# Gathered rows turned on VectorE in 32x32 blocks, odd halves grouped in threes: a mixture-of-experts layer on one Trainium2 core

## The chip, the core and the metric

The kernel runs on one core of a Trainium2 chip. The metric is the time of one execution on the device in microseconds (us); of the kernel before, the median of 9 runs is 820.46. In the text PE is the matrix engine (TensorE) and PEld its weight loads, DVE is VectorE, ACT is ScalarE, POOL is GpSimd and SP is SyncE.

## What is computed

Eight sequences of 512 tokens with 256 features pass one cross-attention and one mixture of experts. Everything is fp32. Cut to what matters:

```
x = x + tanh(g_xattn) * attention(layernorm(x), ctx, ctx, mask)      # 16 heads of 16
x_flat = layernorm(x).reshape(4096, 256)
probs = softmax(x_flat @ router_w + router_b)                        # 8 experts
top_w, top_idx = top_k(probs, 2)
for e in range(8):
    h = gelu(x_flat @ expert_up[e].T)                                # 256 -> 1024
    out_e = h @ expert_down[e].T                                     # 1024 -> 256
    output = output + comb[:, e:e+1] * out_e                         # comb: top_w where e was chosen, else 0
x = x + tanh(g_ffn) * output
```

Each token goes to two experts, so 8,192 rows have to be taken through an expert's two matmuls.

## The kernel before

**Attention first, experts behind it.** `attend_near` takes the eight sequences (batches) one after the other; four stages per batch, each in three parts, hold the attention's steps, and `plan` and `amid` place other work into them by hand. After a batch's attention its rows are normalised and written to a DRAM tensor `rows`, the sum so far goes to `out` (L309 and L312), the router's top two are found (L319 to L356), and `place` (L370 to L390, on POOL) works out for each token the line of a DRAM `table` that it goes to. `enter` (L394) writes the entries with eight indirect DMAs per batch, two per 128 tokens. The table has a share for each expert, filled from its beginning.

**Groups.** A half is 128 rows of one expert, that is 128 lines of the table. A job is a group of halves that one expert works on: a pair (256 rows) or a single (128 rows). Jobs 0 to 4 are full pairs that exist after batch 3 and jobs 5 to 16 full pairs that exist after batch 6. Then come 15 pairs and, after every third of them up to four times, a single that takes an expert's odd last half. `plan` (L642 to L692, small DVE operations) works out which expert and which line each job has, before any of them runs. `JOBS` lists 36 jobs that always run, `MAIN` of them; `compute_extra` holds up to four more singles under a condition that is read at the end.

**One job.** `list_rows` (L712, SP) reads the job's token numbers and weights out of the table. `load` (L724 and L725, SP) brings the expert's two weight matrices, 1 MB each, in one of three buffers. `fetch` (L730, POOL) gathers the rows of the tokens, one indirect DMA per half, into `xg`. `turn` (L746) transposes them on PE, four transposes of 128x128 for a pair, into a PSUM bank, and DVE copies the bank to `xT` (L748). `go_up` (L758) multiplies by the up weights, and ACT applies Gelu (L762) into `hT`. `fetch_y` (L730 as well) gathers what `out` holds for these tokens. `go_down` (L776) multiplies by the down weights, one half at a time, DVE adds the weighted result to the gathered rows (L779), and POOL scatters them back to `out` (L782). As a token's second expert must see the first one's sum, a job's gather from `out` waits until the scatters of the job before have landed.

**Order.** A matmul of fp32 shows as two records in the trace. Jobs 0 to 3 and the turn of job 4 are placed by hand into batches 4 to 7 (`amid`). From job 4 on `compute` writes out the steps of a job s: the row gather of job s+2, the `out` gather of job s-1, the way up of s in four parts, the turn of s+1, the way down of s-1, the listing of s+3 and the load of s+2. The last job does its own way down at the end. After each step one step is taken from a queue with what is left of batches 6 and 7: the projection, the normalisation, the routing, `place`, `enter` and the plans. Within these dependences a scheduler orders each engine's instructions; the ones marked as kept stay in the program's order. Engines and queues then run in order.

The code before:

Of the kernel before, what the change touches and what calls it, by code (L numbers as in the profile page):

```python
# [35 lines left out]

TOKENS = B * S
GROUP = 2 * P
PAIRS = 2 * TOKENS // GROUP
SINGLES = E  # L40

TABLE = TOKENS // GROUP


PARTS = (3, 6, B, B)
ENDS = [-(-(b * S * 2 - E * (GROUP - 1)) // GROUP) for b in PARTS[:2]] + [PAIRS]
SIZES = [ENDS[0], ENDS[1] - ENDS[0], ENDS[2] - ENDS[1], SINGLES]

OFTEN = SINGLES // 2

TABLES = E * TABLE + SIZES[2]

# [3 lines left out]
for _n in range(SIZES[2]):  # L56
    JOBS.append((2, _n))
    if _n % 3 == 2 and _n // 3 < OFTEN:
        JOBS.append((3, _n // 3))
MAIN = len(JOBS)  # L60
JOBS += [(3, n) for n in range(OFTEN, SINGLES)]
# [3 lines left out]
def flamingo_layer(ctx: ExitStack, tc: tile.TileContext, a: dict, out: bass.AP):  # L65
# [11 lines left out]
    table = tc.dram_tile([TABLES * GROUP, ENTRY], I32, name="table")  # L77

    table_parts = dram_disjoint_views(table, B * QT * 2)
    out_parts = dram_disjoint_views(out, 2)  # L80
# [73 lines left out]
    def clear_table(t):  # L154

        many = t.rearrange("p (n c) -> p n c", c=ENTRY)[:, : TABLES * GROUP // P // 11]
        nc.gpsimd.memset(many, 0)
        nc.gpsimd.memset(many[:, :, 0], TOKENS)
        nc.gpsimd.memset(many[:, :, 1], TOKENS - 1)
        n = many.shape[1]  # L160
        nc.sync.dma_start(
            out=table.rearrange("(p r n) c -> p r (n c)", p=P, n=n),
            in_=t[:, : n * ENTRY].unsqueeze(1).to_broadcast([P, TABLES * GROUP // P // n, n * ENTRY]),
        )
# [8 lines left out]
    full_i = mk.tile([P, 2 * TABLE], I32, tag="full_i", name="full_i")  # L173
    nc.gpsimd.iota(full_i, pattern=[[P, 2 * TABLE]], base=0, channel_multiplier=0)
    full = fixed([P, 2 * TABLE], "full")
# [13 lines left out]
    nc.vector.tensor_scalar(filled, iota, float(TOKENS), None, ALU.mult)  # L189
# [422 lines left out]
    def experts(pool, seen, half_bank, bank, row_bank):  # L612
# [6 lines left out]
        tables, loaded, fetched, turned, made, ys = {}, {}, {}, {}, {}, {}  # L619

        def halves(s):
            return 1 if JOBS[s][0] == 3 else 2

        def plan(k):
            n = SIZES[k]
            single = k == 3
            w = 1 if single else 2
            lines = 2 * TABLE // w

            def planned(shape, name, dtype=F32):  # L630
                return plans.tile(shape, dtype, tag=f"{name}{k}", name=f"{name}{k}")

            def scratch(shape, name):
                return plans.tile(shape, F32, tag=name, name=f"{name}{k}")

            def count():

                count = scratch([P, E], "count")
                nc.vector.scalar_tensor_tensor(count, iota, -float(TOKENS), filled, ALU.mult, ALU.add)  # L642
                if not single:
                    nc.vector.tensor_scalar(count, count, 1.0 - GROUP if k < 2 else -float(P), None, ALU.add)
                more = scratch([P, E, lines], f"more{lines}")
                nc.vector.tensor_tensor(
                    more, count.unsqueeze(2).to_broadcast([P, E, lines]),
                    full[:, ::w].unsqueeze(1).to_broadcast([P, E, lines]), ALU.is_gt,
                )
                groups = scratch([P, E + 1], "groups")  # L650
                nc.vector.memset(groups[:, E:], 0.0)
                nc.vector.tensor_reduce(groups[:, :E], more, AX.X, ALU.add)
                if k:
                    nc.vector.scalar_tensor_tensor(groups, tables["done"], -2.0 / w, groups, ALU.mult, ALU.add)
                ahead = scratch([P, E + 1, E], "ahead")
                nc.vector.tensor_tensor(
                    ahead, lower, groups[:, :E].unsqueeze(1).to_broadcast([P, E + 1, E]), ALU.mult
                )
                begin = scratch([P, E + 1], "begin")
                nc.vector.tensor_reduce(begin, ahead, AX.X, ALU.add)  # L660

                line = scratch([P, E + 1], "line")
                nc.vector.scalar_tensor_tensor(line, iota_e, float(lines), begin, ALU.mult, ALU.subtract)
                if k:
                    nc.vector.scalar_tensor_tensor(line, tables["done"], 2.0 / w, line, ALU.mult, ALU.add)
                past = scratch([P, n, E + 1], f"past{n}")
                nc.vector.tensor_tensor(
                    past, slot[:, :n].unsqueeze(2).to_broadcast([P, n, E + 1]),  # L670
                    begin.unsqueeze(1).to_broadcast([P, n, E + 1]), ALU.is_ge,
                )
                whose = scratch([P, n], f"whose{n}")
                nc.vector.tensor_reduce(whose, past, AX.X, ALU.add)
                whose_i = planned([P, n], "whose_i", I32)
                nc.vector.tensor_scalar(whose_i, whose, -1.0, float(E - 1), ALU.add, ALU.min)
                nc.vector.tensor_tensor(past, past, line.unsqueeze(1).to_broadcast([P, n, E + 1]), ALU.mult)
                far = scratch([P, n], f"far{n}")
                nc.vector.tensor_reduce(far, past, AX.X, ALU.max)
                line_i = planned([P, n], "line_i", I32)  # L680
                nc.vector.tensor_tensor(line_i, far, slot[:, :n], ALU.add)
                tables[k] = (whose_i, line_i, planned([P, n, w, FIELDS], "listed", I32))
                if single:
                    tables["extra"] = planned([P, 1], "extra", I32)
                    nc.vector.tensor_scalar(tables["extra"], begin[:, E:], float(OFTEN), None, ALU.is_gt)
                else:
                    done = planned([P, E + 1], "done")
                    nc.vector.tensor_scalar(done, begin, -1.0, float(n), ALU.mult, ALU.add)
                    nc.vector.tensor_scalar(done, done, 0.0, None, ALU.max)
                    nc.vector.tensor_tensor(done, done, groups, ALU.min)  # L690
                    if k:
                        nc.vector.tensor_tensor(done, done, tables["done"], ALU.add)  # L692
                    tables["done"] = done

            return count
# [11 lines left out]
        def list_rows(s):  # L707
            _, line_i, listed, n = planned_for(s)
            w = halves(s)
            lines = E * 2 * TABLE // w + SIZES[JOBS[s][0]]  # L710
            line = number(line_i, n, lines - 1)
            nc.sync.dma_start(  # L712
                out=listed[:, n],
                in_=table[: lines * w * P].rearrange("(r h p) c -> p r h c", h=w, p=P)[
                    :, bass.ds(line, 1), :, :FIELDS
                ].rearrange("p o h c -> p (o h) c"),
            )
# [16 lines left out]

        def fetch(s):
            xg = gather.tile([P, 2, D], F32, tag="xg", name=f"xg{s}")
            for h in range(halves(s)):
                rows_of(rows, s, h, xg[:, h, :])
            fetched[s] = xg

        def turn(s):
            xg, w = fetched.pop(s), halves(s)
            ps = row_bank(f"x_ps{s}").rearrange("p (c r) -> p c r", c=DC)
            for dc in range(DC):
                for h in range(w):
                    nc.tensor.transpose(ps[:, dc, h * P : (h + 1) * P], xg[:, h, dc * P : (dc + 1) * P], ident)  # L746
            xT = gather.tile([P, DC, GROUP], F32, tag="xT", name=f"xT{s}", bufs=2)
            nc.vector.tensor_copy(xT[:, :, : w * P], ps[:, :, : w * P])  # L748
            turned[s] = xT

        def go_up(s, f):
            up, xT, n = loaded[s][0], turned[s], halves(s) * P
            if f == 0:
                made[s] = hpool.tile([P, FC, GROUP], F32, tag="hT", name=f"hT{s}")
            ps = half_bank(f"h_ps{s}_{f}").rearrange("p (i r) -> p i r", i=2)
            for i in range(2):
                for dc in range(DC):
                    nc.tensor.matmul(  # L758
                        ps[:, i, :n], lhsT=up[:, dc, (f + i) * P : (f + i + 1) * P], rhs=xT[:, dc, :n],
                        start=(dc == 0), stop=(dc == DC - 1),  # L760
                    )
            nc.scalar.activation(made[s][:, f : f + 2, :n], ps[:, :, :n], AF.Gelu)  # L762

        def fetch_y(s):

            ys[s] = gather.tile([P, 2, D], F32, tag="y", name=f"y{s}", bufs=2)
# [20 lines left out]
        def ups(s):  # L787
            return [lambda f=f: go_up(s, f) for f in range(0, FC, 2)]
# [4 lines left out]
        def compute(s, end, first):  # L793
# [4 lines left out]
            steps += ups(s)  # L798
            if s + 1 < end:
                steps.append(lambda: turn(s + 1))  # L800
            if s > first:
                steps += downs(s - 1)
# [8 lines left out]
        def compute_extra():  # L811
            some = nc.values_load(
                tables["extra"][0:1, 0:1], min_val=0, max_val=1, skip_runtime_bounds_check_because="it is a comparison"
            )
            with tc.If(some == 1):
# [627 lines left out]
```

## Time and profile before

| what | value |
|---|---|
| median of 9 runs (lowest to highest) | 820.46 us (816.39 to 826.05) |
| the profiled execution | 816.49 us |
| its span, first to last instruction | 814.7 us |
| mean granted PE clock | 0.976 |
| busy: PE, PEld | 750.9 us (92%), 561.8 us (69%) |
| busy: DVE, ACT, POOL | 320.6 us (39%), 253.9 us (31%), 311.9 us (38%) |
| way up, L758, pairs and singles | 1152 matmul records |
| way down, L776 | 1088 matmul records |
| turns on PE, L746 | 136 transposes |
| row gathers, `out` gathers, scatters on POOL | 68 each |

The profiled execution's own time is 1.8 us more than its span; the median of the runs is 4 us above it. A matmul's busy time is modelled and overlaps with the next, so the time that a run of matmuls really takes is read from the chain of work or from the starts in the timeline. The attention lasts until about 361 us; the last batch's normalisation and routing run until about 389 us beside the first of the jobs from 4 on, and from there on the experts are alone.

### The profile page before, as it was taken

What the parts mean: (1) busy time and instruction counts of PE and PEld (TensorE: products, weight loads), DVE (VectorE), ACT (ScalarE), POOL (GpSimd) and SP (SyncE); (2) the same over time, 40 slices, a digit from 0 to 9 for tenths busy, and PEclk for the clock granted to TensorE, in tenths of its full rate; (3) what the DMA queues carried; (4) which work ended last, traced back from release to release, by engine and by line L of the source; (5) the groups of instructions that cost most, each with busy time, mean ns of one, the idle gap of its engine ahead of it and who ended that gap; (6) DMA issues with size and microseconds to landing.
All of it is one profiled execution on the core that took longest, in us unless ns stands there. A gap on an engine that the chain in (4) does not pass through costs nothing.

```text
span 814.7 us, 11329 instructions
## 1 busy us (share of the span) xinstructions
PE 750.9 (92%) x4090; PEld 561.8 (69%) x4090; DVE 320.6 (39%) x958; ACT 253.9 (31%) x487; POOL 311.9 (38%) x420
## 2 busy tenths in 40 slices
PE   4989989896999999899986999999999999999992
PEld 1443444443465757578875888888898988989881
DVE  6867988789865485442400111111111101111100
ACT  3464646372664344524211111212111121111210
POOL 2030124425363434555463535342444334443331
PEclk9998999899999999999998999999999999999997
DMA  4700102000762230526357665756576675766611
GB/s 156 264 8 3 63 27 82 27 29 29 269 213 93 79 108 26 183 79 193 123 185 256 201 225 187 241 175 215 185 236 197 241 222 183 266 200 211 206 47 37
DMA packets 87910, 121.58 MB, mean 149 GB/s; under 512 B 16798, under 2 KB 71713, under 8 KB 87841
## 3 DMA queue, kind: packets, MB, share of 16 engines
q1 hardware_dynamic: 75184, 93.44, 34.2%
q0 software_dynamic: 11840, 26.76, 10.6%
q8 instruction: 36, 0.59, 0.3%
q10 hardware_dynamic: 816, 0.53, 0.2%
q14 instruction: 34, 0.27, 0.1%
HBM read 101.05 MB, written 20.17 MB: 149 GB/s over the span
## 4 chain that ended last, share of the span: by engine, by line
PE 44%; DMA 3%; issue 2%; POOL 2%; DVE 0%; SPq 0%; POOLq 0%
PE o_ps L776 21%; PE h_ps L758 21%; PE x_ps L746 1%; DMA out<-y,listed 1%; DMA up<-in_upT 1%; POOL table L394 1%; DMA table<-entries,place_i 1%; POOL y L730 1%; DMA y<-out,listed 0%; POOL out L782 0%; POOL xg L730 0%; DMA listed<-table 0%; DVE y L779 0%; POOL filled L371 0%; POOL place L370 0%
## 5 line engine op out<-in xcount | busy, mean ns | idle before, releaser
L776 PE MATMUL o_ps<-down,hT 128*128 128x256 f32 x1088 | 243.5, 382 | 8.1 <-DVE y L779 6.9
L758 PE MATMUL h_ps<-xT,up 128*128 128x256 f32 (+1 forms) x1152 | 243.9, 368 | 3.3 <-DVE tops L890 1.7
L776 PEld LDWEIGHTS o_ps<-down,hT 128*128 128x128 f32 x1088 | 204.9, 191 | 39.6 <-DVE y L779 7.4
L758 PEld LDWEIGHTS h_ps<-xT,up 128*128 128x128 f32 x1152 | 208.1, 190 | 33.8 <-issue 4.7
L762 ACT ACTIVATE hT<-h_ps 128x512 f32<-128x512 f32 (+1 forms) x144 | 82.3, 573 | 359.0 <-PE h_ps L758 359.0
L779 DVE SCALAR_TENSOR_TENSOR y<-o_ps,listed,y 128x256 f32<-128x256 f32 x68 | 32.6, 483 | 262.2 <-DMA y<-out,listed 162.9
L730 POOL DMA_INDIRECT y<-out,listed x68 | 66.3, 974 | 163.9 <-DMA out<-y,listed 130.5
L782 POOL DMA_INDIRECT out<-y,listed x68 | 68.8, 1012 | 90.8 <-DVE y L779 65.0
L890 DVE TENSOR_REDUCE tops<-t_ps 128x4 f32<-128x512 f32 x128 | 79.2, 681 | 13.1 <-PE t_ps L885 13.0
L730 POOL DMA_INDIRECT xg<-rows,listed x68 | 64.9, 954 | 41.6 <-issue 16.5
L920 ACT ACTIVATE n_pT<-w_ps 128x512 f32<-128x512 f32 x128 | 66.9, 597 | 39.0 <-PE w_ps L915 38.9
L394 POOL DMA_INDIRECT table<-entries,place_i x64 | 62.7, 980 | 25.7 <-issue 16.5
L748 DVE COPY xT<-x_ps 128x512 f32<-128x512 f32 (+1 forms) x36 | 23.7, 659 | 115.8 <-PE x_ps L746 115.8
L915 PE MATMUL w_ps<-ql,km 32*128 32x512 f32 x256 | 51.8, 677 | 1.4 <-DVE tops L890 1.4
L954 PE MATMUL proj_ps<-woT,oT 128*128 128x256 f32 x128 | 33.1, 394 | 10.7 <-DVE oT L947 10.7
L885 PE MATMUL t_ps<-k,q 32*128 32x256 f32 x512 | 41.5, 404 | 1.1 <-ACT q L557 0.8
L867 POOL TENSOR_TENSOR x<-x,bo 128x1024 f32<-128x1024 f32 x8 | 18.9, 2370 | 59.3 <-issue 34.0
L885 PEld LDWEIGHTS t_ps<-k,q 32*128 32x128 f32 x512 | 25.8, 184 | 20.8 <-issue 11.8
L954 PEld LDWEIGHTS proj_ps<-woT,oT 128*128 128x128 f32 x128 | 23.2, 192 | 22.0 <-DVE oT L947 12.7
L933 PE MATMUL n_av<-n_pT,nv 128*32 128x512 f32 x256 | 35.8, 633 | 1.7 <-DVE xT L748 1.7
L939 DVE STREAM_TRANSPOSE raw<-n_av 128x512 f32<-128x512 f32 x32 | 22.8, 712 | 32.1 <-PE n_av L933 31.0
L553 PE MATMUL q_ps<-n_xnT,wqT 128*128 128x512 f32 x64 | 33.3, 645 | 0.8 <-ACT n_xnT L282 0.5
(187 smaller groups left out, 542.2 us busy)
## 6 DMA issues: line engine op xcount, KB each, us to landing
up<-in_upT SPq DMA_DIRECT2D x36, 1024.0 KB, 7.7
down<-in_downT SPq DMA_DIRECT2D x36, 1024.0 KB, 6.2
out<-x SPq DMA_DIRECT2D x8, 512.0 KB, 3.2
rows<-xn_f SPq DMA_DIRECT2D x8, 512.0 KB, 3.6
x<-in_x SPq DMA_DIRECT2D x7, 512.0 KB, 6.9
table<-none SPq DMA_DIRECT2D x1, 2288.0 KB, 12.1
xg<-rows,listed POOLq DMA_INDIRECT x68, 4.4
y<-out,listed POOLq DMA_INDIRECT x68, 2.8
```

The costliest lines, as they stand in the source:

```text
L394: nc.gpsimd.indirect_dma_start(out=table_parts[2 * t + i][:, :], out_offset=bass.IndirectOffsetOnAxis(ap=place_i[:, t, i : i + 1], axis=0) ...
L730: nc.gpsimd.indirect_dma_start(out=dst, out_offset=None, in_=src[: seen[JOBS[s][0]], :], in_offset=bass.IndirectOffsetOnAxis(ap=listed[:, ...
L758: nc.tensor.matmul(ps[:, i, :n], lhsT=up[:, dc, (f + i) * P : (f + i + 1) * P], rhs=xT[:, dc, :n], start=(dc == 0), stop=(dc == DC - 1),)
L762: nc.scalar.activation(made[s][:, f : f + 2, :n], ps[:, :, :n], AF.Gelu)
L776: nc.tensor.matmul(ps, lhsT=hT[:, f, h * P : (h + 1) * P], rhs=down[:, f, :], start=(f == 0), stop=(f == FC - 1))
L782: nc.gpsimd.indirect_dma_start(out=out_parts[h][:, :], out_offset=bass.IndirectOffsetOnAxis(ap=listed[:, n, h, 0:1], axis=0), in_=y[:, h, ...
L885: ins = nc.tensor.matmul(ps[j][:, u], lhsT=q[rows_j, c, t * P : (t + 1) * P], rhs=k[rows_j, c], start=True, stop=True)
L890: nc.vector.tensor_reduce(top[:, 2 * tp : 2 * tp + 2, :].rearrange("p t (i x) -> p t i x", i=2)[:, :, :, 32 * j], ps[j], AX.X, ALU.max,)
L915: ins = nc.tensor.matmul(ps[j], lhsT=km[rows_j, c, i, :], rhs=lowered[b, c][rows_j, i, :], start=True, stop=True)
L920: nc.scalar.activation(pT[:, j, :], ps[j], AF.Exp)
L933: ins = nc.tensor.matmul(av[32 * j : 32 * j + 32, :], lhsT=made_of(b)[3][:, 8 * c + 2 * j + r, :], rhs=pT[:, j, :], start=True, stop=True,)
L954: nc.tensor.matmul(ps[:, t - ts[0], :], lhsT=outs[b, c][:, t * P : (t + 1) * P], rhs=w["woT"][:, c, :], start=(c == 0), stop=(c == DC - 1),)
```

## The change

**Turns.** From job 4 on rows are no longer transposed on PE. `turn_block` uses DVE's transpose, which turns blocks of 32x32. A step i reads 32 partitions of `xg` and does four transposes that write to the four groups of 32 partitions of `xT`; the access patterns put each block at its place in the transposed matrix. Four such steps, 16 instructions, turn a job's rows from SBUF to SBUF. In `compute` they stand one behind each part of the way up. Jobs 0 to 3 keep the turn on PE.

**Groups of three.** The singles are gone. Of the rows that are left after job 16, an expert with an odd number of halves and at least two pairs left gives its last three halves as a triple (384 rows); at most four triples, the rest in pairs. `JOBS` has 32 jobs that always run: 5 + 12 pairs as before, then 11 pairs with a triple after the second, fifth, eighth and eleventh; seven more pairs stand under conditions. A triple's way up takes eight parts of one 128-row weight block by 384 columns. A triple has buffers of its own (`wide`), in memory that the attention's buffers leave when the queue of leftover steps is empty. The table becomes one list of lines of 128 rows, with a share of 33 per expert, and a job reads two or three lines from wherever it begins. The plans are rewritten for this; the third and fourth become one, `plan_rest`.

**The last job.** Its way up is split: a quarter of it, then the way down of the job before, then the rest, then its own way down.

The diff, cut:

```diff
-PAIRS = 2 * TOKENS // GROUP
-SINGLES = E
-PARTS = (3, 6, B, B)
-SIZES = [ENDS[0], ENDS[1] - ENDS[0], ENDS[2] - ENDS[1], SINGLES]
-OFTEN = SINGLES // 2
+TRIPLES = 4
+HALVES = TOKENS // P
+SHARE = HALVES + 1
+PARTS = (3, 6, B)
+SIZES = [ENDS[0], ENDS[1] - ENDS[0], TRIPLES, 2 * TOKENS // GROUP + E - 1 - TRIPLES - ENDS[1]]
+OFTEN = SIZES[3] - 7
+MORE = OFTEN + 3
+LINES = E * SHARE + 2 * SIZES[3]
...
-for _n in range(SIZES[2]):
-    JOBS.append((2, _n))
-    if _n % 3 == 2 and _n // 3 < OFTEN:
-        JOBS.append((3, _n // 3))
+for _n in range(OFTEN):
+    JOBS.append((3, _n))
+    if _n % 3 == 1 and _n // 3 < TRIPLES:
+        JOBS.append((2, _n // 3))
...
         def halves(s):
-            return 1 if JOBS[s][0] == 3 else 2
+            return 3 if JOBS[s][0] == 2 else 2
...
+        def plan_rest():
+            count = count_rows(2)
...
+            nc.vector.tensor_reduce(pairs, more[:, 0], AX.X, ALU.add)
+            nc.vector.tensor_reduce(whole, more[:, 1], AX.X, ALU.add)
+            left, odd = each("left"), each("odd")
+            nc.vector.tensor_tensor(left, pairs, tables["done"][:, :E], ALU.subtract)
+            nc.vector.tensor_tensor(odd, pairs, whole, ALU.subtract)
+            three = each("three")
+            nc.vector.scalar_tensor_tensor(three, left, 2.0, odd, ALU.is_ge, ALU.mult)
...
+        def turn_block(s, i):
+            w = halves(s)
+            if i == 0:
+                where, bufs = (wide[0], 1) if w == 3 else (gather, 2)
+                turned[s] = where.tile([P, DC, w * P], F32, tag="xT" if w == 2 else "xT3", name=f"xT{s}", bufs=bufs)
+            src = fetched[s].rearrange("p h (k g x) -> p g k h x", k=DC, x=32)
+            dst = turned[s].rearrange("p k (h i r) -> p i k h r", h=w, r=32)
+            for g in range(4):
+                nc.vector.transpose(dst[32 * g : 32 * g + 32, i], src[32 * i : 32 * i + 32, g])
...
-        def go_up(s, f):
+        def go_up(s, f, m):
...
-            ps = half_bank(f"h_ps{s}_{f}").rearrange("p (i r) -> p i r", i=2)
-            for i in range(2):
+            ps = half_bank(f"h_ps{s}_{f}")[:, : m * n].rearrange("p (i r) -> p i r", i=m)
+            for i in range(m):
...
         def ups(s):
-            return [lambda f=f: go_up(s, f) for f in range(0, FC, 2)]
+            m = 512 // (halves(s) * P)
+            return [lambda f=f: go_up(s, f, m) for f in range(0, FC, m)]
+        def turns(s):
+            return [lambda i=i: turn_block(s, i) for i in range(4)]
...
-            steps += ups(s)
+            up = ups(s)
+            last = downs(s - 1) if s > first else []
             if s + 1 < end:
-                steps.append(lambda: turn(s + 1))
-            if s > first:
-                steps += downs(s - 1)
+                turned_next = turns(s + 1)
+                for step in up:
+                    steps += [step, *turned_next[:1]]
+                    turned_next = turned_next[1:]
+                steps += turned_next + last
+            else:
+                steps += up[:2] + last + up[2:]
...
-            + [lambda: load(5), lambda: turn_rows(4)],
+            + [lambda: load(5), *turns(4)],
...
                 if queue:
                     queue.popleft()()
+                    if not queue:
+                        heads.close()
+                        open_wide()
```

## The prediction

> **What bounds the kernel now.** I read the profiled execution first by the page's busy shares, then by stage, then along the chain of work that ended last. The execution took 816.49 us: its span of 814.7 and 1.8 around it. The median shown is 820.46, so sums are made on 816.49 and the same difference is taken off the median.
>
> The page says that PE is busy for 92% of the span. An average hides where the rest is, so the next view is the busy time by stretch (columns: stretch; its length; PE, PEld, DVE, ACT and POOL busy with their counts; granted clock; DMA share; GB/s):
>
> ```profile
> 400.00:427.00 27.00, 25.30 (x120) 21.72 (x119) 6.84 (x33) 4.18 (x7) 16.08 (x17) 1.00 0.48 151
> 427.00:441.33 14.33, 7.59 (x37) 6.50 (x37) 0.54 (x2) 2.39 (x4) 5.58 (x6) 0.87 1.03 361
> 441.33:785.20 343.87, 343.87 (x1693) 304.39 (x1694) 40.10 (x75) 58.08 (x103) 140.06 (x143) 1.00 0.61 203
> ```
>
> From 441.33 to 785.20 PE never stops: 343.87 of 343.87 us at clock 1.00, with DVE 12% busy. This is the expert stage once the attention is over. Before it lies a hand-over with holes. The same stretch in the chain of work (start, length, what) has PE instructions alone:
>
> ```profile
> 578.30 6.91 PE h_ps L758 x32
> 585.20 0.22 PE x_ps L746 x2
> 585.42 6.91 PE o_ps L776 x32
> 592.33 3.57 PE h_ps L758 x32
> 595.90 0.44 PE x_ps L746 x4
> ```
>
> A pair's way up and its way down cost 6.91 us each. The turn that stands between them costs 0.44 (0.22 for a single half). A single's way up costs 3.57, more than half of 6.91, because its 32 weight loads serve 128 columns each. Here every microsecond taken off PE shortens the run, as long as nothing else falls behind it.
>
> **Turns off PE, steady stretch.** From job 4 on `turn` becomes `turn_block`. After 441.33 the chain holds 21 turns at 0.44 and 4 at 0.22: 9.2 + 0.9 = **10.1 us removed**.
>
> **Triples for singles.** The plan changes from 32 pairs and 4 singles to 28 pairs and 4 triples: 68 halves both times. I counted each expert's rows from the inputs: 6, 9, 6, 10, 8, 9, 11 and 9 halves. Four experts have an odd half and at least two pairs left, so each of the four triples is full, and 11 pair groups remain for the 11 places. The conditional groups behind them are skipped, as now. PE's columns stay the same; only the short matmuls go. One up matmul record takes 6.91 / 32 = 0.216 us at 256 columns and 3.57 / 32 = 0.112 at 128, so by the same slope 0.320 at 384 and 10.25 for a triple's way up. Four pairs and four singles cost 4 x (6.91 + 3.57) = 41.9, four triples 41.0: **0.9 removed**. Four loads of 2 MB go as well; they are hidden (DMA share 0.61). Of the edits around them none is on the path: a triple's eight Gelus (between 0.38 at 256 columns and 0.60 at 512) lie beside 10.25 us of PE; the table grows from 36,608 to 38,400 rows and is cleared before the first token is routed; the triples' buffers take the attention's memory, but the first is filled some 13 jobs after the attention ends.
>
> **The blocks on DVE.** The rows that price them (mean ns of one after the bar):
>
> ```profile
> L748 DVE COPY xT<-x_ps 128x512 f32<-128x512 f32 x32 | 22.0, 688 | 92.0 <-PE x_ps L746 92.0
> L947 DVE STREAM_TRANSPOSE oT<-n_o 128x512 f32<-128x512 f32 x16 | 11.4, 710 | 0.5
> 398.51 0.29 DVE L646 TENSOR_TENSOR more<-count,full 128x128 f32<-128x128 f32 x1
> ```
>
> A pair's turn loses one copy of 0.69 and gains 16 transposes over 32 partitions, 128 elements deep. No row shows that form. From below, the small DVE operations of the planning take 0.16; from above, a transpose of 512 elements takes 0.71. I take 0.30, from the nearest row by depth, 128 elements in 0.29. That is 4.8 us per pair, between 2.6 and 11.4. A triple's blocks are 192 deep: 0.37 each, between this row and 0.44 for 256 elements, so 5.9 us.
>
> A pair job will last 2 x 6.91 = 13.8 us on PE. DVE then needs 4.8 + 2 x 0.48 for its two `y` additions = 5.8, and 12.4 at the upper bound. So the cost is nothing, hidden by PE's 13.8 us, unless DVE's order matters. The blocks stand in front of `y` of the job before. That `y` waits for a loop on POOL: scatter, landing, gather of the next `y`, landing. In the last jobs it reads: additions start at 778.30, the second at 778.70; the scatters end at 781.70; the gather starts at 783.93 when they have landed; its second half issues at 785.22 and lands 2.74 later (the chain's last y gather) at 787.96. From addition to the next possible addition: 787.96 - 778.70 = 9.3 us. DVE has nothing else to do in that gap, and 4.8 fits. If the cover is gone (blocks over about 9.3 / 16 = 0.58 each), `y` comes late and PE runs out of its two banks.
>
> The Trainium skill speaks against such blocks. "VectorE: DVE Perf Modes", section "Two Vector instructions with no wait between them", says that an instruction whose input or output starts in another group of 32 partitions than the last one's begins only when everything earlier has finished. All 16 blocks change their output group, so by it none overlaps another, while in this trace two additions of 0.48 took 0.88 together. The same page's section on the fixed extra latency gives (N + 151) / 0.96 ns for an fp32 addition of N elements, an estimate of 291 for 128 and 4.7 us for 16 in a row: the sum would not change. No row of this case shows a change of group.
>
> **The hand-over, 340 to 441 us.** Three things move. First, job 4's blocks now run on DVE amid the last attention work. The second half of its rows landed late (its turn is at 350.8, its way up begins at 353.04). With 4.8 us in place of 0.69 the way up can start some 4 later, with other PE work to fill part: +2.5, between 0 and 5. Second, a job now has 14 steps in place of 11, so the queue that is emptied one step per step puts batch 7's routing and its table writes about half a job earlier against PE. The hole that this may close:
>
> ```profile
> 422.51 4.92 DMA up<-in_upT
> 427.43 0.14 issue
> 427.57 7.14 PE h_ps L758 x32
> 434.71 0.45 PE x_ps L746 x4
> 435.16 5.63 issue
> 440.79 0.49 DVE y L779
> 441.33 8.70 PE o_ps L776 x32
> ```
>
> PE idles 0.83, 0.71, 1.55 and 6.18 here, and after the last hole its 32 matmuls take 8.70 instead of 6.91 (clock 0.87 in that stretch): 11.1 in all, plus 7 turns of 0.44. Third, against it: the table writes bunch. POOL has six indirect issues per job at 1.29 (start to start), 7.7 us; placing takes 4.5 and eight table writes 10.3. In one job of 13.8 that is 22.5, so POOL could fall 8.7 behind, and `y` with it. The planning on DVE is as long as before (about 45 small operations in place of 36). From -14 (11.1 and 3.1 gone) to +9 (POOL's lag, with job 4's loss in the same hole); I take **-2**, near the middle.
>
> **The end.** The last group's `y` gather used to wait for the group before. Now that group's way down comes after a quarter of the last way up, and the gather lands behind the other three quarters (7.7 us) and the first half's way down. Two scatters and three gathers on POOL move forward with it, past no other work; SP has nothing left to issue. Today PE ends at 799.03 and the last scatter is issued until 803.35: 4.32. With `y` there: 0.2 + 0.48 + 0.28 + 1.02 = 2.0. If the last two scatters still wait for one addition, 1.3 comes back. So 1.0 to 2.3; I take **-1.7**.
>
> **Sum:** -10.1 - 0.9 - 2 - 1.7 = -14.7 on 816.49, so 801.8 for a profiled execution. The median goes from 820.46 to **805.8**.
>
> **Rivals.**
> 1. The hand-over decides upward: POOL's bunching and job 4 cost +9 in place of -2, so the sum is -3.7 and the median 816.8. For it: a PE hole of 6.18 came from just such a backlog. Against: part of it only replaces the hole that is there. Chance 0.10.
> 2. The hand-over closes: -14, the sum -26.7, median 793.8. For it: the wait at 435 began with a late weight load behind the table writes, which move earlier. Chance 0.12.
> 3. Slower: DVE's order puts the blocks between the arrival of `y` and its addition, so they lengthen the loop. It becomes 9.3 + 16b against today's period of 14.26 (2 x 6.91 + 0.44). It turns slower from b = 0.31 per block, hardly above my 0.30. At b = 0.40 the loop is 15.7, +1.4 against today for some 18 pair jobs, +26, less 2.6 for the end and the triples: about 844. Against: in program order the blocks come before that addition, with a gap of 9.3 for 4.8. Chance 0.08.
> 4. Nothing gained: PE's matmuls stretch by what the turns leave (granted clock below 1.00 in the steady stretch), 820. The clock is 1.00 now with PE fully busy. Chance 0.04.
>
> **How the numbers follow.** The forecast has 0.66. The range reaches to 796, toward case 2, and to 817, with case 1 inside. What is left out is case 3, case 4 and part of case 2, some 0.2. By 0.5% (4.1 us, about what a measurement of this kernel can tell from no change) the bound for faster is 816.4: the forecast, case 2 and half of case 1 give 0.83; the same 0.09 (half of 1 and case 4); slower 0.08.
>
> **What would show it.** Right: no x_ps on PE after job 3; PE busy for the whole stretch after the hand-over; rows of about 0.3 us for 16 blocks per pair; a triple's way up near 10.25; the last scatter about 2 us behind PE's end. Wrong: PE idle behind DVE `y` in steady pair jobs, or DVE `y` issued late behind xT blocks (rival 3); new holes before the steady stretch (rival 1).

## The result and the profile after

The kernel after takes **859.45 us** (median of 20 runs, 854.03 to 865.87) against 822.72 for the kernel before (62 runs): a ratio of 1.0445, 95% interval 1.0422 to 1.0468. It is slower, where 805.8 was forecast. The profiled execution has a span of 860.2 against 814.7. The profiled execution of before, 816.49, lies near its fastest run (816.39) and 6 us under its median, so a difference between two profiles can be some 6 us off from one between medians.

The busy time by stretch of the kernel after; first the stretch shown of before, then two parts of it (columns as there):

```profile
441.33:785.20 343.87, 307.17 (x1327) 257.95 (x1326) 125.37 (x378) 52.39 (x92) 130.87 (x134) 0.95 0.52 173
443.60:554.00 110.40, 110.40 (x513) 97.17 (x512) 46.87 (x146) 19.11 (x32) 47.97 (x50) 1.00 0.63 210
554.00:785.20 231.20, 194.50 (x805) 158.77 (x804) 76.32 (x225) 33.28 (x60) 82.53 (x85) 0.92 0.48 156
```

PE was busy for all of 343.87 us before and for 307.17 now. The loss has a place: from 443.60 until 554 PE has no hole, although all turns are on DVE there, and after it 36.7 us of holes come in. The groups of the page (mean ns, then idle time before them and what ended it):

```profile
L872 PE MATMUL o_ps<-down,hT 128*128 128x256 f32 x1088 | 253.4, 392 | 38.1 <-DVE y L875 38.1
L843 DVE STREAM_TRANSPOSE xT<-xg 32x128 f32<-32x128 f32 (+1 forms) x448 | 139.8, 312 | 203.2 <-DMA xg<-rows,listed 190.0
```

PE waits for `y`, that is for a PSUM bank that a `y` addition has to free, and DVE waits 190 us for row gathers, in front of its blocks. Idle time of DVE costs nothing by itself; here the two rows are one chain, as rows of PE, DVE and POOL from the timeline around 590 show (start, us, engine, line, what, and in brackets the idle time before and its releaser; other rows are left out):

```profile
588.75 9.73 PE L872 MATMUL o_ps<-down,hT 128*128 128x256 f32 x32 [7.07 <-DVE y L875]
...
590.01 0.48 DVE L875 SCALAR_TENSOR_TENSOR y<-o_ps,listed,y 128x256 f32<-128x256 f32 x1
590.78 1.00 POOL L878 DMA_INDIRECT out<-y,listed  x1 [0.79 <-DVE y L875]
593.99 0.98 POOL L807 DMA_INDIRECT y<-out,listed  x1 [2.21 <-DMA out<-y,listed]
595.28 0.97 POOL L807 DMA_INDIRECT y<-out,listed  x1 [0.30 <-issue]
596.55 0.95 POOL L807 DMA_INDIRECT xg<-rows,listed  x1 [0.30 <-issue]
597.81 0.95 POOL L807 DMA_INDIRECT xg<-rows,listed  x1 [0.30 <-DMA y<-out,listed]
...
601.73 3.77 DVE L843 STREAM_TRANSPOSE xT<-xg 32x128 f32<-32x128 f32 x12 [11.23 <-DMA xg<-rows,listed]
605.54 0.48 DVE L875 SCALAR_TENSOR_TENSOR y<-o_ps,listed,y 128x256 f32<-128x256 f32 x1
606.06 1.26 DVE L843 STREAM_TRANSPOSE xT<-xg 32x128 f32<-32x128 f32 x4
607.35 0.48 DVE L875 SCALAR_TENSOR_TENSOR y<-o_ps,listed,y 128x256 f32<-128x256 f32 x1
```

Read it as a loop. A second addition at 590.01, its scatter, the landing, the gather of the next `y`; then, behind these two on POOL, the row gather of a later job; 11.23 us of DVE waiting for those rows; twelve blocks; and only then the next `y`, at 605.54, though its own gather had been issued by 596.3 (in this stretch such gathers land 2.8 us after their issue, so its rows were there by about 599). From one second addition to the next it is 607.35 - 590.01 = 17.3 us, and PE makes a pair in 13.8. The order in which DVE's instructions stand in the compiled kernel says why (xT19x12: twelve of job 19's blocks; y15: one addition of job 15, y14*2: two; 19 is the first triple; the kernel "late blocks" is one of the experiments below, with its blocks held in the program's order):

```
after        xT17x16 y14*2 xT18x16 xT19x2 y15 xT19x12 y15 xT19x2 xT20x12 y16 xT20x4 y16 xT21x12 y17
late blocks  xT17x16 y15*2 xT18x16 y16*2 xT19x16 y17*2 xT20x16 y18*2 xT21x16 y19*3
```

The second line has the program's order: job 18's blocks stand behind `y` of job 15. The scheduler put them ahead of it. With two `xT` buffers it could run one job ahead. A triple has a third buffer, `xT3`, and from there on it ran two ahead: job 20's blocks stand before `y` of job 16, and on POOL job 20's row gather stands behind job 16's `y` gather. The Trainium skill ("PSUM — Partial Sum Buffer", section "Engine vs sequencer instructions") calls VectorE's and GpSimd's queues strict first in, first out. The rows above agree: the addition starts 0.04 us after the twelfth block's end, and not when its data is there.

That is **theory A: the loss is the wait for rows that was put in front of an earlier `y`**, not the time of the blocks. Its rivals: the blocks cost by their own time on DVE (rival 3 of the prediction), or the triples or the hand-over cost.

### The profile page after: what moved, and what is told of

It reads as the page before. It is cut to its first block, busy times and chain, and to the rows that moved or that the text cites. A ratio compares the mean times of both kernels' runs of the same rounds, so it can differ in the third digit from the quotient of the medians.

```text
span 860.2 us, 11151 instructions
## 1 busy us (share of the span) xinstructions
PE 758.2 (88%) x3842; PEld 546.0 (63%) x3842; DVE 444.1 (52%) x1384; ACT 253.9 (30%) x487; POOL 312.1 (36%) x420
## 5 line engine op out<-in xcount | busy, mean ns | idle before, releaser
L872 PE MATMUL o_ps<-down,hT 128*128 128x256 f32 x1088 | 253.4, 392 | 38.1 <-DVE y L875 38.1
L872 PEld LDWEIGHTS o_ps<-down,hT 128*128 128x128 f32 x1088 | 213.3, 197 | 77.7 <-DVE y L875 41.2
L843 DVE STREAM_TRANSPOSE xT<-xg 32x128 f32<-32x128 f32 (+1 forms) x448 | 139.8, 312 | 203.2 <-DMA xg<-rows,listed 190.0
L854 PEld LDWEIGHTS h_ps<-xT,up 128*128 128x128 f32 x1024 | 195.3, 192 | 44.7 <-DVE tops L1007 3.2
L1032 PE MATMUL w_ps<-ql,km 32*128 32x512 f32 x256 | 56.9, 692 | 2.5 <-DVE tops L1007 1.4
L1071 PE MATMUL proj_ps<-woT,oT 128*128 128x256 f32 x128 | 35.0, 410 | 10.7 <-DVE oT L1064 10.7
L1071 PEld LDWEIGHTS proj_ps<-woT,oT 128*128 128x128 f32 x128 | 23.9, 198 | 24.0 <-DVE oT L1064 12.7
```

The source lines that it names most:

```text
L843: nc.vector.transpose(dst[32 * g : 32 * g + 32, i], src[32 * i : 32 * i + 32, g])
L854: nc.tensor.matmul(ps[:, i, :], lhsT=up[:, dc, (f + i) * P : (f + i + 1) * P], rhs=xT[:, dc, :], start=(dc == 0), stop=(dc == DC - 1),)
L872: nc.tensor.matmul(ps, lhsT=hT[:, f, h * P : (h + 1) * P], rhs=down[:, f, :], start=(f == 0), stop=(f == FC - 1))
L1032: ins = nc.tensor.matmul(ps[j], lhsT=km[rows_j, c, i, :], rhs=lowered[b, c][rows_j, i, :], start=True, stop=True)
L1071: nc.tensor.matmul(ps[:, t - ts[0], :], lhsT=outs[b, c][:, t * P : (t + 1) * P], rhs=w["woT"][:, c, :], start=(c == 0), stop=(c == DC - 1),)
```

## The experiments

They ran on three chips with the kernel before beside them (medians 822.8, 821.4 and 837.6), so ratios to before are compared. Two edits make a table of four kernels: whether the blocks are held in the program's order, and whether they begin with job 4 or with job 10.

**Blocks held in order** (all of after, with one line):

```diff
-                nc.vector.transpose(dst[32 * g : 32 * g + 32, i], src[32 * i : 32 * i + 32, g])
+                ins = nc.vector.transpose(dst[32 * g : 32 * g + 32, i], src[32 * i : 32 * i + 32, g])
+                tc.keep_in_program_order(ins)
```

> The changed kernel with one addition: every block transpose is kept in the program's order on DVE, behind whatever DVE instruction was written before it. Theory A (run-ahead): the scheduler put a later job's blocks in front of an earlier job's y addition (xT20 in front of y16, and so on), and those blocks wait for a row gather that POOL issues only after that y's own gather; so y waits for a gather that it does not need. With the order kept, xT(s+2) stands in front of y(s) and its rows have long landed. A expects the 49 us of holes behind 554 us and most of the hand-over's hole of 9.6 us to go: about 803 us, between 797 and 810, PE without a hole from about 445 us to its end. Theory B (the blocks' own cost: 16 x 0.315 us per job on DVE, and what they take from other engines) expects no change, 850 to 860. Theory C (a triple's three gathers and three scatters make the loop over out too long) expects the holes near the triples to stay: about 8 us at each of the four, 830 to 840.

Measured: 815.68 us, ratio 0.9916 (0.9892 to 0.9940). The loss is gone with the order alone: the same instructions, the same buffers, 5.1% less time. In the stretch of the first table PE has no hole any more:

```profile
441.33:785.20 343.87, 343.87 (x1534) 291.10 (x1533) 136.22 (x413) 59.88 (x106) 146.96 (x151) 1.00 0.57 188
```

A's 797 to 810 was too low by the hand-over, which in these profiles is 8.7 us longer than before (way down of job 10 at 480.30, before 471.62). The two rivals' times, 830 and more, are ruled out.

**Rows that needn't be waited for.** After, in the scheduler's order, but the late blocks read a constant tile; the rows are still fetched. The diff, cut (the tile `still`, filled once, is `wide[1]`):

```diff
...
-            src = fetched[s].rearrange("p h (k g x) -> p g k h x", k=DC, x=32)
+            src = wide[1][:, :w, :] if s > 18 else fetched[s]
+            src = src.rearrange("p h (k g x) -> p g k h x", k=DC, x=32)
```

> The kernel after, but from job 19 on the blocks read a constant tile in place of the group's gathered rows, so the rows are still fetched but nothing waits for them; it leaves out the true rows of these groups. Triples' blocks still stand in front of earlier y additions and as many blocks run on DVE. Theory A (what costs is the wait for the row gather in front of y): no wait of PE for y from 560 on, PE without a hole there, median 812 to 826. Theory B (the blocks' own time or their order on DVE costs, whatever they wait for): 845 to 860.

Measured: 813.12 us, 0.9894 (0.9862 to 0.9926). Its groups:

```profile
L847 DVE STREAM_TRANSPOSE xT<-still 32x128 f32<-32x128 f32 (+1 forms) x208 | 67.2, 323 | 82.1 <-PE h_ps L858 79.3
L876 PE MATMUL o_ps<-down,hT 128*128 128x256 f32 x1088 | 243.1, 382 | 2.1 <-DVE y L879 2.1
```

The 208 late blocks run as long as ever (323 ns in the mean; 324 by the means of the two forms in the kernel after) and still stand ahead of earlier additions. The scheduler even moved some further ahead, job 19's to between the additions of job 4. But PE's wait for `y` falls from 38.1 to 2.1 us. So neither the blocks' time nor their place costs; the wait that they bring to that place does: 1.0445 - 0.9894 = 5.5%, some 45 us.

**Two buffers for the late jobs.** After, but jobs 17 to 31 share two `xT` buffers of triple size, so a triple gives no third one.

```diff
-                where, bufs = (wide[0], 1) if w == 3 else (gather, 2)
-                turned[s] = where.tile([P, DC, w * P], F32, tag="xT" if w == 2 else "xT3", name=f"xT{s}", bufs=bufs)
+                late = 17 <= s < MAIN
+                turned[s] = (wide[0] if late else gather).tile(
+                    [P, DC, w * P], F32, tag="xT3" if late else "xT", name=f"xT{s}", bufs=2
+                )
```

> The changed kernel, nothing kept in order, but from job 17 on pairs and triples share two xT buffers (in the changed kernel a triple has a third of its own). The third buffer is what theory A takes for the trigger: with it the scheduler can place blocks one job further ahead. With two, DVE's order has xT(s+3) in front of y(s) nearly throughout, and those rows are gathered a job earlier than y's. A expects the holes behind 560 us to go but for those at the change of buffers (jobs 17 and 18), and the hand-over to stay as in the changed kernel, about 7 us behind the kernel before: 809 to 820. B expects 850 to 860, C 830 to 840.

Measured: 821.84, 0.9984 (0.9954 to 1.0014), a little above A's 809 to 820. Around the change of buffers, where for two jobs there are more than two, PE waits 10.1 us for `y` (three holes, the longest 7.2); from 560 to 790 it has none. In the compiled order job 20's blocks now stand behind `y` of job 16. The number of buffers set how far the scheduler ran ahead.

**Blocks from job 10 on, held in order.** Jobs 4 to 9 are turned on PE as before.

```diff
+EARLY = 10
...
+                if s + 1 < EARLY:
+                    steps += up + [lambda: turn(s + 1)] + last
...
-            + [lambda: load(5), *turns(4)],
+            + [lambda: load(5), lambda: turn_rows(4)],
```

> The kernel after with job 4 to 9 turned on PE as before (with their copies), and the blocks of the jobs from 10 on held at their place in the program's order. Theory A (the loss is blocks put in front of an earlier y; blocks that stay behind it cost nothing): the hand-over is as long as before, the steady stretch keeps the 9.9 us that the pinned kernel gained there, and the end gives 0.2 to 0.6. PE ends near 789, span 803 to 807, median 807 to 813. If blocks in the hand-over were not what made the pinned kernel lose 8.7 us there (the triples' plan or the longer queue of steps did), it stays at 814 to 817.

Measured: **805.12 us, 0.9784 (0.9747 to 0.9821)**, faster than both kernels and a little better than expected in the median (expected was 807 to 813; the profiled execution, the slowest of the six, has a span of 807.6, just over the expected 803 to 807). That 805.1 lies beside the forecast's 805.8 is luck: it is another kernel, and the forecast's terms missed in both directions, as shown below. PE's busy time by stretch from the end of the hand-over, and DVE in that stretch:

```profile
444.82:785.00 340.18, 340.18 (x1501) 287.07 (x1502) 132.83 (x402) 58.71 (x104) 144.23 (x147) 0.99 0.56 183
```
```profile
592.63 0.48 DVE L877 SCALAR_TENSOR_TENSOR y<-o_ps,listed,y 128x256 f32<-128x256 f32 x1 [8.28 <-PE o_ps L874]
596.09 0.48 DVE L877 SCALAR_TENSOR_TENSOR y<-o_ps,listed,y 128x256 f32<-128x256 f32 x1 [2.97 <-PE o_ps L874]
596.49 5.04 DVE L844 STREAM_TRANSPOSE xT<-xg 32x128 f32<-32x128 f32 x16
606.45 0.48 DVE L877 SCALAR_TENSOR_TENSOR y<-o_ps,listed,y 128x256 f32<-128x256 f32 x1 [4.92 <-PE o_ps L874]
```

This is what the prediction drew: additions that wait for PE alone, and sixteen blocks in the gap behind them.

**Blocks from job 10 on, in the scheduler's order** (the kernel above without the held order).

> The kernel of the late blocks with the blocks left where the scheduler puts them; from job 15 on that is the same order as in the kernel after. Theory A: the whole loss of the triples' section (46 us between the kernel after and the one whose blocks wait for no rows) is there without any block in the hand-over: median 847 to 855, PE waiting for y some 40 us. If the loss needs the hand-over's lag as well, 815 to 840.

Measured: 1.0338 (1.0269 to 1.0406) on the chip where before takes 837.6. Against the 0.9784 of the held order it is the same loss, some 46 us, and it is there without the blocks of jobs 4 to 9. PE's waits from 441 to 860:

```profile
PE o_ps L873 <- DVE y L876: 36.4, 7, 8.2
```

**Blocks from job 7 on, held in order** (10 becomes 7).

> The kernel of the late blocks with blocks from job 7 on in place of job 10. If the pinned kernel's 8.7 us in the hand-over come from job 4 to 6 (blocks beside the last attention work on DVE), this one gains the three turns of 0.44 and lies 0 to 2 below the late blocks'. If they come from the longer queue of steps (14 a job in place of 11, table writes earlier), it loses 3 to 8 of them again.

Measured: 0.9801 (0.9751 to 0.9851), the same as from job 10 on. So the hand-over's loss comes with jobs 4 to 6, not with the three more steps per job in jobs 7 to 9. Whether it is their blocks, which meet the last attention work, or their own three more steps per job, which move the table writes, this kernel does not separate.

| ratio to before | in the scheduler's order | in the program's order |
|---|---|---|
| blocks from job 4 on | 1.0445 (after) | 0.9916 |
| blocks from job 10 on | 1.0338 | 0.9784 |

The columns differ by 0.053 and 0.055, the rows by 0.011 and 0.013: two separate losses that add up, as far as the intervals tell. 1.0445 = 0.9784 + 0.054 (rows in front of `y`, 45 us) + 0.012 (hand-over, 10 us).

**Blocks alone and triples alone.** Before with blocks from job 4 on and its pairs and singles; and the plan of the change with every turn on PE, without the split.

> The kernel before with the blocks on DVE from job 4 on and nothing else: pairs and singles as before, two xT buffers, the last job's way up in one part, order left to the scheduler. Theory A expects the 10 us of turns gone from the steady stretch and the hand-over about 7 us worse, since two buffers don't let the blocks run ahead of y far enough: 814 to 823. Theory B (the blocks' own cost) expects most of the loss here: 845 to 860. Theory C expects what A expects, there being no triples.

> The changed plan with triples, but every turn on PE as in the kernel before (a triple's in two PSUM banks) and the last job's way up in one part. Theory A expects nothing to stand in front of y, so the time of before less some 1 us: 815 to 824. Theory B the same. Theory C expects the loss here: 845 to 855.

Measured: 1.0014 (0.9982 to 1.0046) and 0.9947 (0.9915 to 0.9980). Blocks alone are no loss: without triples there is no third buffer, and what they gain in the steady stretch the hand-over (PE waits 9.52 us for `y` there) and later holes (5.4 us in four, the longest, 3.61, behind a single) take. The triples are worth 4.3 us (1.6 to 7.0), not 0.9.

**The split alone**, on the kernel before:

```diff
-            steps += ups(s)
-            if s + 1 < end:
-                steps.append(lambda: turn(s + 1))
-            if s > first:
-                steps += downs(s - 1)
+            up = ups(s)
+            last = downs(s - 1) if s > first else []
+            if s + 1 < end:
+                steps += up + [lambda: turn(s + 1)] + last
+            else:
+                steps += up[:2] + last + up[2:]
```

> The kernel before with one edit: the group before the last goes down after a quarter of the last group's way up. With a single condition behind it, the forecast's term of the end in full: PE's end to the last scatter falls from 4.3 to 1.8 to 3.3, the exit stays at 11.4, the span falls by 1.0 to 2.5 and the median by as much (ratio 0.997 to 0.999). If the exit grows by what the scatter gains, no change.

Measured: 0.9994 (0.9963 to 1.0026), no change. The last scatter does move to 2.5 us behind PE's end (4.3 before), but then 12.85 pass until the span ends, where 11.35 did. This profile also shows what singles cost, in PE's timeline around one:

```profile
694.96 3.73 PE L758 MATMUL h_ps<-xT,up 128*128 128x128 f32 x32
698.53 0.60 PE L746 MATMUL x_ps<-ident,xg 128*128 128x128 f32 x4
701.79 7.17 PE L776 MATMUL o_ps<-down,hT 128*128 128x256 f32 x32 [2.66 <-DVE y L779]
```

A single is over in half the time, its neighbours' `y` loop is not, and PE waits 2.66 us. The profiled execution of before has no such hole, this one and that of the blocks alone (3.61 at 698.71) do.

**Three kernels for the end**, all variants of the late blocks: one condition around the extra pairs in place of two nested ones; none (the extra pairs' code is left out, which these inputs skip); and the last way up in one piece.

> The kernel of the late blocks with one condition around all seven extra pairs in place of two nested ones. If the second condition costs at the exit: the time from the last scatter's end to the span's end falls from 13.4 to about 11.4, and the median is 1.5 to 2.0 us below the late blocks'. If the exit differs for another reason (DMAs of the triples' parts, the third view of the output), it stays at 13 to 13.7 and the median is the same within 0.5.

> The kernel of the late blocks without the conditional extra pairs (it leaves out the code of the groups that these inputs skip). PE's end to the span's end lay between 14.8 and 15.9 in all the kernels so far, while the last scatter's end moved by 2.5 against it. If the way past the skipped code is what bounds the end, PE's end to the span's end falls below 13 and the median by 2 or more; if something that follows any program's end does, it stays at 14.8 to 15.9 and the median is the same as the late blocks' within 1.

> The kernel of the late blocks with the last group's way up in one piece again. From the split alone, which gained nothing on the kernel before (0.9994): PE's end to the last scatter grows from 1.8 to about 2.6 to 4.3, PE's end to the span's end stays between 14.8 and 15.9, the median is the same as the late blocks' within 1.5.

Measured: 0.9792 (0.9753 to 0.9831) for one condition, with 13.47 from the last scatter to the span's end as against 13.05 for two: the nesting is not it. 0.9798 (0.9748 to 0.9847) without the split: no gain shows here either. Without any condition the last matmuls and the last scatter, in a span of 816.1:

```profile
796.42 10.52 PE L874 MATMUL o_ps<-down,hT 128*128 128x256 f32 x48
```
```profile
807.74 0.98 POOL L880 DMA_INDIRECT out<-y,listed  x1 [2.44 <-POOLq L1499]
```

and the same two of the blocks from job 7 on, in a span of 818.3:

```profile
792.73 10.52 PE L874 MATMUL o_ps<-down,hT 128*128 128x256 f32 x48
```
```profile
804.05 0.98 POOL L880 DMA_INDIRECT out<-y,listed  x1 [2.45 <-DVE y L877]
```

From PE's end to the span's end it is 816.1 - 806.94 = 9.2 without the condition and 818.3 - 803.25 = 15.1 with it. With the condition it is 15.1 after and 15.7 before, whatever the last scatter does. So in these profiles the way past the skipped code, and not the scatter, bounds the end: the 2 us that the scatter won were hidden beside it. The median does not show the 5.9 us (0.9798, interval 0.9748 to 0.9847, four runs); what takes them back there, or whether the spread hides them, stays open.

## Why the prediction was wrong, step by step

**What bounds the kernel: right.** PE bounds the steady stretch, and in the kernel of the late blocks it still does, with no hole.

**Turns off PE, -10.1: right.** From the way down of job 10 to PE's end it was 799.03 - 471.62 = 327.4 before and 797.84 - 480.30 = 317.5 with the blocks held in order: 9.9 less. In that stretch the forecast takes off 19 x 0.44 + 4 x 0.22 = 9.2 for turns and 0.9 for triples.

**Blocks of 0.30: right.** A pair's sixteen take 5.04 us, 0.315 from start to start; a triple's 6.11 (forecast 5.9). By the Trainium skill's rule ("VectorE: DVE Perf Modes", section "Two Vector instructions with no wait between them") none of them overlaps another, and the rows agree: they run one behind another, 0.315 apart at 0.303 each. The prediction's estimate from that page's formula for an fp32 addition was 0.291.

**"So the cost is nothing, hidden by PE's 13.8 us, unless DVE's order matters": this step failed.** It counted DVE's busy time against PE's period and took DVE's order from the program: "in program order the blocks come before that addition, with a gap of 9.3 for 4.8." But only marked instructions keep the program's order, and the new ones weren't marked. The change took the reader of the row gather off PE and gave it to the engine that also carries `y`. With that, a transfer that had held nothing up became a part of `y`'s loop, which went from the 9.3 of the prediction to 17.3. Rival 3 named the right engine, loop and sign at 0.08, with the wrong price: 16 x b for the blocks, where the runs show a wait for a landing. Its rule that the loss begins at b = 0.31 falls with the kernel that reads a constant tile.

**Triples, -0.9: right sign, too small.** Alone they measured -4.3 (1.6 to 7.0). The term priced PE's matmuls and left out the holes behind singles. That these are the rest is argued from two profiles, not measured. A triple's way up takes 10.32 us (forecast 10.25). In after the triples were also what opened the third buffer.

**Hand-over, -2 between -14 and +9: too low.** By the table's rows, against blocks from job 10 on, it is +9 to 11, at the upper end. (Single profiles say less: job 10's way down begins 6.7 us later in after and 8.7 later with the blocks held, but it also lies 7.1 apart in the late blocks with two conditions and with one.) In after the largest hole has the same cause as those of the steady stretch: job 7's sixteen blocks wait 13.85 us for rows, in front of job 4's `y`:

```profile
391.38 5.09 DVE L843 STREAM_TRANSPOSE xT<-xg 32x128 f32<-32x128 f32 x16 [13.85 <-DMA xg<-rows,listed]
396.51 0.88 DVE L875 SCALAR_TENSOR_TENSOR y<-o_ps,listed,y 128x256 f32<-128x256 f32 x2
```

PE, whose next matmul waits for that `y`, idles for 9.59 until 397.05. With the blocks held in order these are PE's longest waits from 340 to 443.6:

```profile
PE h_ps L855 <- DMA up<-in_upT: 6.8, 1, 6.8
PE h_ps L855 <- DVE xT L843: 5.4, 2, 2.8
```

The second is the prediction's "+2.5, between 0 and 5" for job 4, once for job 4 and once for job 5: job 4's blocks begin at 357.26, right behind an addition that waited 5.66 us for PE, and job 5's stand amid the last attention work, where DVE is busy for 17.37 of the 20 us from 360. The first stands behind the bunched table writes that the prediction foresaw. All eight are issued in a row on POOL; the listing on SP that waits for them follows, then the weight load, and PE has its weights at 427.39:

```profile
409.99 1.07 POOL L396 DMA_INDIRECT table<-entries,place_i  x1 [0.53 <-POOL place_i L392]
...
418.95 0.96 POOL L396 DMA_INDIRECT table<-entries,place_i  x1 [0.30 <-issue]
...
421.24 0.37 SPq L791 DMA_DIRECT2D listed<-table  x1
422.35 0.37 SPq L801 DMA_DIRECT2D up<-in_upT  x1
```

The writes also stand eight in a row in after and in the blocks alone; before, and with blocks from job 7 or job 10 on, scatters and gathers come between them. So rival 1, bunching and job 4 at +9, given 0.10, is near what the held order shows. That the bunching costs the 6.8 is read from the traces; no run tried it alone.

**The end, -1.7: nothing.** The scatter moved as forecast, from 4.3 to 1.8 behind PE's end, but the span's end stayed 15.1 us behind PE's end (15.7 before). The step failed in taking the scatter for what ends the span.

**The sum.** With the blocks where the prediction believed them and none before job 10, the change gives -16 us (medians 805.1 and 821.4 on one chip) where -10.1 - 0.9 - 1.7 = -12.7 was forecast for those parts.

## What to carry to other kernels

Work that moves to another engine brings its waits along: before "that engine is 39% busy, so it's free", ask what the moved instruction waits for, what will stand behind it in that queue, and whether the bottleneck waits for that. Where a scheduler orders the queues, the program's order isn't the queue's order, and an extra buffer is leave to run one job further ahead; hold the new instructions in place, or keep the buffers scarce. A share of 343.87 in 343.87 says what there is to win; a loop's length (9.3 against 13.8) says how much wait it can take in before that is lost.

## What was unexpected of the hardware

After a long hole PE is slow: the 32 matmuls behind the 7.07 us hole take 9.73 us as against 7.07 in the steady stretch, and the granted clock over 554 to 785 is 0.92. Not every hole does it: those behind the 2.66 us one of the split alone take 7.17. So 36.7 us of holes cost some 45.

A condition whose code is skipped costs at the end: from PE's last matmul to the span's end it is 15.1 us with it and 9.2 without, in one profile each; the medians did not show the gain.
